# Layer 2 of a four-layer kernel: rows 0 and 32 of the spectrum packed into one, two columns per transform over h

## The chip, the core and the metric

The kernel runs on one core of a Trainium2 chip. The core has a matrix engine, TensorE (PE in the profile; PEld is its loading of stationary operands), a vector engine, VectorE (DVE), a scalar engine, ScalarE (ACT), GpSimd (POOL) and SyncE (SP), which issues most transfers. Each engine works through its own instructions in order and waits for the others by semaphores. Working data lie in SBUF, in 128 partitions; PE writes to PSUM, [...]and another engine copies the result from there. The metric is the device time of one execution in microseconds (us).

## The reference, cut to what matters

Four layers follow one another, each of the form x = x + L(group norm of x), on x of shape (2, 128, 64, 64) in float32: layer 0 has two attentions, layer 1 convolutions, layer 2 a quaternion convolution in the spectrum, layer 3 an attention. The change is in layer 2 alone:

```python
xs = jnp.stack([x[:, :q], x[:, q:2 * q], x[:, 2 * q:3 * q], x[:, 3 * q:]])
Xs = jnp.fft.rfft2(xs, s=(64, 64), axes=(-2, -1))
Ws = jnp.stack([kr_w + 1j * ki_w, kr_x + 1j * ki_x, kr_y + 1j * ki_y, kr_z + 1j * ki_z])
C = jnp.einsum('piohw,qbihw->pqbohw', Ws, Xs)
Pw = C[0, 0] - C[1, 1] - C[2, 2] - C[3, 3]
...
P = jnp.stack([Pw, Px, Py, Pz])
o = jnp.fft.irfft2(P, s=(64, 64), axes=(-2, -1))
```

Here q is 32. The spectrum has 64 rows (frequencies over h) and 33 columns (over w). Each of its points has its own 32x32 matrices, in eight arrays, so the layer reads 67.6 MB of weights.

## The kernel before

Layer 2 is `_layer2`. Each engine keeps the order in which the program issues (`_in_order`). There are three stages.

**Stage A, the transforms over h.** For each of the two images, `columns(i)` takes four columns of x: ACT normalizes them into `g` (L825), PE transposes two at a time (L831), DVE copies the result into `gt` (L837). `transformed(i, gt)` multiplies by `k["fwd_h"]` (L843), which makes, for each column, cosine and sine sums for rows 0 to 32 of the spectrum: 66 numbers. DVE copies them into `y` (L850), a tile that holds both images as (row, cosine or sine, column). `_skewed` issues the first function for group i+1 ahead of the second for group i.

**Stage B, the blocks.** As x is real, the transform over h of row 64 - m is the conjugate of that of row m, so 33 rows serve for all 64. Eight blocks (`kb`) take four rows each, and each block has two halves: the products with the weights of rows m (direct) and with those of rows 64 - m (image). `spectra(kb)` names the block's rows; the last block has five, as row 32 has only a direct half and row 0 only an image half. For a row, `transposed` has PE turn `y` (L872) and ACT copy it to `yt` (L878), and the second `transformed` multiplies by `k["fwd_w_both"]` (L885), which gives the transform over w for both halves. `placed` copies these to the tile `e` of a half with the signs of the quaternion product: twelve small copies per row, on ACT for one of two rows (L914) and on DVE for the other (L916). `products` multiplies by the weights (L975): 17 steps of four products on 32 columns of PE each. DVE transposes the results (L984) and adds them into `pz` (L992). `turned` transposes `pz` (L1004) and copies it to `pzt` on ACT (L1011), and `back` transforms back over w (L1027 and L1030, L1039 for row 0), with DVE's copies to `y` (L1032, L1040), where the results replace the inputs.

`alongside` runs one half's `products` and, between its steps, a queue of side work: generators that issue a piece each time they are called. In the first half of a block the queue is `turned` for the image half of the block before, `back` for that block, and `begun`: the first two rows of the next block, copied to its image tile only. In the second half it is `ended`: the same two rows copied to the direct tile, `turned` for the direct half, and the other rows into both tiles. The weights of a half are two transfers of 2112 KB on SP's queue (L789) into one of two buffers, so they are issued when the half two before has ended. The tiles of PSUM with the tag `bank` have two buffers, shared by `transposed`, `turned`, `back` and the last product step.

**Stage C, the transforms back over h.** `turned_back(i)` has PE transpose `y` for four columns (L1117), each to 66 partitions, and ACT copies to `zt` (L1124). `added(i, zt)` multiplies by `k["inv_h"]` (L1130), 66 rows by 64 columns, and DVE adds to x (L1134). In the second image, the statistics of the first image for layer 3 are made alongside: `steps` issues one piece per group (L1351 and the lines after).

Of the kernel before, what the change touches and what calls it, by code (L numbers as in the profile page):

```python
# [18 lines left out]
CH = 512  # L19
# [10 lines left out]
def _blocks():  # L30
# [11 lines left out]
    ang = 2 * np.pi * np.outer(np.arange(H), np.arange(FH)) / H  # L42
    k["fwd_h"] = np.kron(np.eye(2), np.concatenate([np.cos(ang), -np.sin(ang)], 1))
# [3 lines left out]
    k["fwd_w_both"] = np.zeros((2, W, 2, FW + 1, 2))  # L47
    for image, sign in enumerate((1, -1)):
        k["fwd_w_both"][0, :, image, :FW, 0] = c
        k["fwd_w_both"][0, :, image, :FW, 1] = -s  # L50
        k["fwd_w_both"][1, :, image, :FW, 0] = sign * s
        k["fwd_w_both"][1, :, image, :FW, 1] = sign * c
    k["fwd_w_both"] = k["fwd_w_both"].reshape(2 * W, 4 * (FW + 1))
# [4 lines left out]
    inv = np.stack([np.concatenate([c, s], 1), np.concatenate([-s, c], 1)], 1).reshape(2 * FW, 2 * W)  # L58
    k["inv_w"] = inv
    k["inv_w_mirror"] = inv * np.repeat([1.0, -1.0], W)  # L60

    ang = 2 * np.pi * np.outer(np.arange(FH), np.arange(H)) / H
    k["inv_h"] = np.stack([np.cos(ang), -np.sin(ang)], 1).reshape(2 * FH, H) / (H * W)
# [705 lines left out]
def _layer2(ctx, tc, X, weights, cst, src, here=None, there=None):  # L769
# [24 lines left out]
    y = one.tile([128, B, FH, 2, W], F32, name="y")  # L794
    with tc.tile_pool(name="l2_a", bufs=3) as ap, tc.tile_pool(
# [18 lines left out]
        for b in range(B):  # L814
# [8 lines left out]
            def columns(i):  # L823
                g = ap.tile([128, 4, H], F32, name="g")
                nc.scalar.activation(  # L825
                    g, xw[:, 4 * i : 4 * i + 4, :], AF.Identity, bias=shift, scale=scale
                )
                next(steps, None)
                pt = aps.tile([128, CH], F32, tag="pt", name="ps_pt")
                for n in range(2):  # L830
                    nc.tensor.transpose(  # L831
                        pt[:, n * 128 : (n + 1) * 128],
                        g[:, 2 * n : 2 * n + 2, :].rearrange("p w h -> p (w h)"),
                        ident,
                    )
                gt = ap.tile([128, 256], F32, name="gt")
                nc.vector.tensor_copy(gt, pt[:, :256])  # L837
                return gt

            def transformed(i, gt):  # L840
                py = aps.tile([128, CH], F32, tag="py", name="ps_py")
                for n in range(2):
                    nc.tensor.matmul(  # L843
                        py[:, n * 4 * FH : (n + 1) * 4 * FH],
                        gt[:, n * 128 : (n + 1) * 128],
                        k["fwd_h"],
                        start=True,
                        stop=True,
                    )
                nc.vector.tensor_copy(  # L850
                    y[:, b, :, :, 4 * i : 4 * i + 4].rearrange("p f c w -> p w c f"),
                    py[:, : 8 * FH].rearrange("p (w c f) -> p w c f", w=4, c=2),
                )

            _skewed(columns, transformed, W // 4)

    two = ctx.enter_context(tc.tile_pool(name="l2_two", bufs=2))
    with tc.tile_pool(name="l2_e", bufs=3) as ep, tc.tile_pool(
# [6 lines left out]
        def spectra(kb):  # L865

            return [4 * kb + 1 + j for j in range(4)] + [0] * (kb == BLOCKS2 - 1)

        def transposed(m):
            pt = bank()  # L870
            for b in range(B):
                nc.tensor.transpose(  # L872
                    pt[:, b * 128 : (b + 1) * 128],
                    y[:, b, m, :, :].rearrange("p c w -> p (c w)"),
# [6 lines left out]
        def transformed(yt):  # L881

            pe = bank("pe")
            for b in range(B):
# [3 lines left out]
                    k["fwd_w_both"],  # L888
# [5 lines left out]
        def placed(kb, m, got, image, e, scalar):  # L894
# [3 lines left out]
            if image:  # L898
                if m == FH - 1:
                    return  # L900
                s, row = (1, 4 * kb + 4 - m) if m else (0, 0)
            else:
                if not m:
                    return
                s, row = 0, m - 4 * kb - 1
# [31 lines left out]
        def rows_in(kb, rows, places, es, yts=None):  # L937

            if yts is None:
                yts = [transposed(m) for m in rows]  # L940
                yield
            gots = [transformed(yt) for yt in yts]
# [75 lines left out]
        def back(kb, direct, image):  # L1018

            for b in range(B):  # L1020
                pq = bank()
                for j in range(4):
                    m = 4 * kb + 1 + j
                    both = m != FH - 1
                    to = pq[:, j * 128 : (j + 1) * 128]
                    lhs = direct[b][:, j].rearrange("p r o -> p (r o)")
                    nc.tensor.matmul(to, lhs, k["inv_w"], start=True, stop=not both)  # L1027
                    if both:
                        lhs = image[b][:, 3 - j].rearrange("p r o -> p (r o)")
                        nc.tensor.matmul(to, lhs, k["inv_w_mirror"], start=False, stop=True)  # L1030
                m = 4 * kb + 1
                nc.vector.tensor_copy(  # L1032
                    y[:, b, m : m + 4, :, :].rearrange("p m c w -> p (m c w)"), pq
                )
                yield
                if kb == BLOCKS2 - 1:
                    pq = bank()
                    lhs = image[b][:, 0].rearrange("p r o -> p (r o)")
                    nc.tensor.matmul(pq[:, :128], lhs, k["inv_w"], start=True, stop=True)  # L1039
                    nc.vector.tensor_copy(  # L1040
                        y[:, b, 0, :, :].rearrange("p c w -> p (c w)"), pq[:, :128]
                    )
                    yield
# [1215 lines left out]
```

## Time and profile before

The times of three runs and of the profiled execution:

| what | us |
|---|---|
| median of three runs | 4382.42 |
| the three runs | 4372.78 to 4385.77 |
| the profiled execution | 4377.08 |
| its span, first to last instruction | 4375.3 |
| layer 2, stage A (1962.38 to 1999.92) | 37.5 |
| layer 2, stage B (2000 to 2278.85) | 278.9 |
| layer 2, stage C (2278.85 to 2359.60) | 80.8 |

The rest of the span belongs to the other three layers. The profile gives, for each engine, the time it was busy, the time it was idle before an instruction, and which instruction of which engine released it. PE's clock is not constant: the profile has the share of full clock that was granted, and shows it per window. A float32 product appears as two records of PE (two passes), a transpose as one.

```profile
PE 4128.4 (94%) x35988; PEld 1595.2 (36%) x35988; DVE 2203.8 (50%) x2410; ACT 3353.7 (77%) x4080; POOL 68.0 (2%) x145
PEclk9999999999999999999985999999999999999999
```

The second of these lines has one digit per fortieth of the span, in tenths of full clock; the digits 8 and 5 at the twenty-first and twenty-second place are layer 2's stage C and its neighbours.

### The profile page before, as it was taken

What the parts mean: (1) busy time and instruction counts of PE and PEld (TensorE: products, weight loads), DVE (VectorE), ACT (ScalarE), POOL (GpSimd) and SP (SyncE); (2) the same over time, 40 slices, a digit from 0 to 9 for tenths busy, and PEclk for the clock granted to TensorE, in tenths of its full rate; (3) what the DMA queues carried; (4) which work ended last, traced back from release to release, by engine and by line L of the source; (5) the groups of instructions that cost most, each with busy time, mean ns of one, the idle gap of its engine ahead of it and who ended that gap; (6) DMA issues with size and microseconds to landing.
All of it is one profiled execution on the core that took longest, in us unless ns stands there. A gap on an engine that the chain in (4) does not pass through costs nothing.

```text
span 4375.3 us, 82819 instructions
## 1 busy us (share of the span) xinstructions
PE 4128.4 (94%) x35988; PEld 1595.2 (36%) x35988; DVE 2203.8 (50%) x2410; ACT 3353.7 (77%) x4080; POOL 68.0 (2%) x145
## 2 busy tenths in 40 slices
PE   6899999979999997988887999999999999999998
PEld 3422222245222224445566333333333333333332
DVE  3579999736899998987753111222122212211111
ACT  3378888734888884226442999999999999999998
POOL 1001000000000001000000000000000000000000
PEclk9999999999999999999985999999999999999999
DMA  9996000000000000004640000000000000000000
GB/s 213 191 192 88 1 1 1 1 1 2 1 1 1 1 1 7 1 24 185 272 160 8 4 6 6 4 6 6 6 4 6 6 6 6 4 6 6 6 6 4
DMA packets 158826, 158.67 MB, mean 36 GB/s; under 512 B 24810, under 2 KB 148714, under 8 KB 154355
## 3 DMA queue, kind: packets, MB, share of 16 engines
q1 hardware_dynamic: 158450, 153.27, 14.8%
q8 instruction: 284, 4.65, 0.4%
q14 instruction: 92, 0.75, 0.1%
HBM read 144.85 MB, written 73.40 MB: 50 GB/s over the span
## 4 chain that ended last, share of the span: by engine, by line
PE 82%; DVE 13%; ACT 3%; issue 1%; POOL 0%; DMA 0%; SPq 0%; DVEq 0%; ACTq 0%; POOLq 0%
PE ps_acc L2057 23%; PE ps_s L2038 19%; PE ps_s L1313 13%; PE ps_acc L1726 12%; DVE X L649 4%; PE ps_sp L1517 4%; PE ps_z L975 2%; DVE sums L1761 1%; DVE e L916 1%; PE ps_po L1130 1%; PE ps_sp L1495 1%; PE ps_acc L1992 1%; ACT weights L1322 1%; PE ps_pt L1117 1%; PE ps_acc L1966 1%
## 5 line engine op out<-in xcount | busy, mean ns | idle before, releaser
L2048 ACT ACTIVATE weights<-ps_s 128x1024 f32<-128x1024 f32 x2048 | 1888.0, 1086 | 64.3 <-PE ps_s L2038 61.5
L1322 ACT ACTIVATE weights<-ps_s 128x1024 f32<-128x1024 f32 x1024 | 992.5, 1022 | 174.1 <-PE ps_s L1313 149.1
L2057 PE MATMUL ps_acc<-weights,vt 128*32 128x512 f32 x8192 | 1094.3, 606 | 0.0
L2038 PE MATMUL ps_s<-q,k 32*128 32x512 f32 x8192 | 932.6, 446 | 8.9 <-ACT weights L2048 8.9
L1761 DVE TENSOR_TENSOR sums<-sums,weights 128x2048 f32<-128x2048 f32 x384 | 879.1, 2289 | 42.1 <-ACT weights L1322 6.2
L2038 PEld LDWEIGHTS ps_s<-q,k 32*128 32x128 f32 x8192 | 472.5, 183 | 848.9 <-ACT weights L2048 788.6
L1313 PE MATMUL ps_s<-q,k 32*128 32x512 f32 x4096 | 645.8, 641 | 3.6 <-ACT weights L1322 2.2
L2079 DVE COPY u<-ps_acc 128x512 f32<-128x512 f32 x32 | 22.1, 691 | 1066.3 <-PE ps_acc L2057 1066.3
L1726 PE MATMUL ps_acc<-weights,vt 128*32 128x512 f32 x4096 | 548.9, 605 | 3.4 <-ACT used L1751 3.2
L1313 PEld LDWEIGHTS ps_s<-q,k 32*128 32x128 f32 x4096 | 209.7, 183 | 429.8 <-issue 212.5
L2057 PEld LDWEIGHTS ps_acc<-weights,vt 128*32 128x32 f32 x8192 | 163.0, 108 | 380.0 <-issue 368.0
L1726 PEld LDWEIGHTS ps_acc<-weights,vt 128*32 128x32 f32 x4096 | 81.0, 108 | 395.7 <-issue 377.6
L649 DVE SCALAR_TENSOR_TENSOR X<-g,w,X 128x2048 f32<-128x2048 f32 x84 | 197.3, 2350 | 2.4
L1517 PE MATMUL ps_sp<-pad,diag 32*32 32x512 f32 x4608 | 172.2, 609 | 11.2 <-issue 5.6
L1761 DVE TENSOR_TENSOR sums<-weights 128x2048 f32<-128x2048 f32 x64 | 146.5, 2289 | 61.4 <-ACT weights L1322 61.4
L1999 DVE TENSOR_TENSOR vt<-ps_acc,bv 128x384 f32<-128x384 f32 x32 | 17.8, 557 | 293.3 <-PE ps_acc L1992 293.3
L975 PE MATMUL ps_z<-w_ri,e 128*32 128x128 f32 x2048 | 138.1, 407 | 10.3 <-DVE e L916 5.3
L1517 PEld LDWEIGHTS ps_sp<-pad,diag 32*32 32x32 f32 x4608 | 93.5, 104 | 77.6 <-issue 32.5
L1495 PE MATMUL ps_sp<-xn,w_qkv 128*128 128x512 f32 x160 | 89.2, 695 | 32.6 <-DVE k L1528 15.2
L2082 DVE RECIPROCAL r<-r 128x512 f32<-128x512 f32 x32 | 107.3, 3353 | 1.1
L914 ACT ACTIVATE e<-ps_pe 32x136 f32<-32x136 f32 (+1 forms) x363 | 102.0, 281 | 4.2
L916 DVE TENSOR_SCALAR e<-ps_pe 32x136 f32<-32x136 f32 (+1 forms) x341 | 101.1, 297 | 4.7
(290 smaller groups left out, 2689.3 us busy)
## 6 DMA issues: line engine op xcount, KB each, us to landing
w_ri<-w_r SPq DMA_DIRECT2D x16, 2112.0 KB, 8.1
w_ri<-w_i SPq DMA_DIRECT2D x16, 2112.0 KB, 13.4
w_r<-in_L_conv_kr_w SPq DMA_DIRECT2D x15, 528.0 KB, 12.4
w_r<-in_L_conv_kr_x SPq DMA_DIRECT2D x15, 528.0 KB, 12.1
w_r<-in_L_conv_kr_y SPq DMA_DIRECT2D x15, 528.0 KB, 12.0
w_r<-in_L_conv_kr_z SPq DMA_DIRECT2D x15, 528.0 KB, 12.1
w_i<-in_L_conv_ki_w SPq DMA_DIRECT2D x15, 528.0 KB, 12.4
w_i<-in_L_conv_ki_x SPq DMA_DIRECT2D x15, 528.0 KB, 11.9
```

The source lines that it names most:

```text
L649: nc.vector.scalar_tensor_tensor(xi, g[:, i : i + H // 2, j : j + W], w8[:, s : s + 1], xi, ALU.mult, ALU.add)
L916: nc.vector.tensor_scalar_mul(out, got[of, :, s], sign)
L975: nc.tensor.matmul(out.rearrange("p (n f o) -> p n f o", n=2, f=2), e[:, s, 2 * j : 2 * j + 2, :].rearrange("p f x -> p (f x)"), w.rearran ...
L1313: nc.tensor.matmul(ps[j // 2][:, j % 2, :], k[rows, kt * 128 : (kt + 1) * 128], q[rows, qb * CH : (qb + 1) * CH], start=True, stop=True,)
L1322: nc.scalar.activation(w[:, 2 * p : 2 * p + 2, :], ps[p], AF.Exp)
L1495: nc.tensor.matmul(ps[:, i // ROWS, : rows * W], w_qkv[:, grp * C : (grp + 1) * C], xn[:, (first + r0 + i) * W : (first + r0 + i + rows) * W],
L1517: nc.tensor.matmul(ps[r // 2][to, r % 2, :].rearrange("p (h w) -> p h w", w=W), diag[rows, grp, t, :], pad[rows, y0 : y0 + ROWS, t % 3 : t ...
L1726: nc.tensor.matmul(ac[n][rows, :], lhs(rows), w[:, j, :], start=first, stop=last)
L1761: nc.vector.tensor_add(parts[0].rearrange("p j c -> p (j c)"), t.rearrange("p j c -> p (j c)"), w.rearrange("p j c -> p (j c)"),)
L2038: nc.tensor.matmul(ps[j // 2][:, j % 2, :], k[rows, kt * 128 : (kt + 1) * 128], q[n][rows, qb * CH : (qb + 1) * CH], start=(n == 0), stop= ...
L2048: nc.scalar.activation(w[p], ps[p], AF.Exp)
L2057: nc.tensor.matmul(ac[0][32 * j : 32 * j + 32, :], vt[:, kt, j // 2, i : i + 2, :].rearrange("p a d -> p (a d)"), w[j // 2][:, i, :], star ...
```

## The change

Rows 0 and 32 are real after the transform over h: their sines vanish. So they share one place. `fwd_h` now makes 64 numbers per column: row 0's cosine sum, row 32's in the place of row 0's sine, and cosine and sine for rows 1 to 31. Two columns fill 128 partitions, both on the way there and on the way back. `y` becomes (column, cosine or sine, row), with 32 rows.

The groups of stages A and C take eight columns in place of four, `steps` is called twice per group, and the copy to `y` in stage A goes to ACT. In stage B every block has four rows. The packed one is number 0; it has its own matrix forward (`fwd_w_ends`) and two on the way back (`inv_w_32`, `inv_w_0`). Each half now prepares two rows of the next block, for both tiles, ahead of `turned` and `back`; `e` has four buffers for three. The copies to `y` in `back` go to ACT, one per image and block, two in the last block.

```diff
-    k["fwd_h"] = np.kron(np.eye(2), np.concatenate([np.cos(ang), -np.sin(ang)], 1))
+    over_h = np.stack([np.cos(ang), -np.sin(ang)], 1)
+    over_h[:, 1, 0] = np.cos(np.pi * np.arange(H))
+    k["fwd_h"] = np.kron(np.eye(2), over_h.reshape(H, H))
...
+    k["inv_h"] = np.kron(np.eye(2), over_h.reshape(H, H).T / (H * W))
...
-    y = one.tile([128, B, FH, 2, W], F32, name="y")
+    y = one.tile([128, B, W, 2, FH - 1], F32, name="y")
...
-                g = ap.tile([128, 4, H], F32, name="g")
+                g = ap.tile([128, 8, H], F32, name="g")
                 nc.scalar.activation(
-                    g, xw[:, 4 * i : 4 * i + 4, :], AF.Identity, bias=shift, scale=scale
-                )
-                next(steps, None)
+                    g, xw[:, 8 * i : 8 * i + 8, :], AF.Identity, bias=shift, scale=scale
+                )
+                for _ in range(2):
+                    next(steps, None)
...
-                for n in range(2):
+                for n in range(4):
                     nc.tensor.transpose(
...
-                gt = ap.tile([128, 256], F32, name="gt")
-                nc.vector.tensor_copy(gt, pt[:, :256])
+                gt = ap.tile([128, CH], F32, name="gt")
+                nc.vector.tensor_copy(gt, pt)
...
-                nc.vector.tensor_copy(
-                    y[:, b, :, :, 4 * i : 4 * i + 4].rearrange("p f c w -> p w c f"),
-                    py[:, : 8 * FH].rearrange("p (w c f) -> p w c f", w=4, c=2),
-                )
-
-            _skewed(columns, transformed, W // 4)
+                for n in range(4):
+                    cols = slice(n * 128, (n + 1) * 128)
+                    nc.tensor.matmul(py[:, cols], gt[:, cols], k["fwd_h"], start=True, stop=True)
+                nc.scalar.copy(
+                    y[:, b, 8 * i : 8 * i + 8, :, :].rearrange("p w c f -> p (w c f)"), py
+                )
+
+            _skewed(columns, transformed, W // 8)
...
-    with tc.tile_pool(name="l2_e", bufs=3) as ep, tc.tile_pool(
+    with tc.tile_pool(name="l2_e", bufs=4) as ep, tc.tile_pool(
...
-            return [4 * kb + 1 + j for j in range(4)] + [0] * (kb == BLOCKS2 - 1)
+            return [(4 * kb + 1 + j) % (FH - 1) for j in range(4)]
...
-                    y[:, b, m, :, :].rearrange("p c w -> p (c w)"),
+                    y[:, b, :, :, m].rearrange("p w c -> p (w c)"),
...
-                    k["fwd_w_both"],
+                    k["fwd_w_both" if m else "fwd_w_ends"],
...
-                nc.vector.tensor_copy(
-                    y[:, b, m : m + 4, :, :].rearrange("p m c w -> p (m c w)"), pq
-                )
+                for lo, hi in ((0, 4),) if kb < BLOCKS2 - 1 else ((0, 3), (3, 4)):
+                    m = (m0 + lo) % (FH - 1)
+                    nc.scalar.copy(
+                        y[:, b, :, :, m : m + hi - lo].rearrange("p w c m -> p (w c) m"),
+                        pq[:, lo * 128 : hi * 128].rearrange("p (m x) -> p x m", m=hi - lo),
+                    )
...
+            side, n = [], 0
+            if nxt:
+                side.append(rows_in(kb + 1, nxt[:2], (1, 0), es))
+                n += 8
             if before:
-                side, n = [turned(pzs[1], before[1]), back(kb - 1, *before)], 7
+                side += [turned(pzs[1], before[1]), back(kb - 1, *before)]
+                n += 6
             else:
-                side, n = [rows_in(0, first[i : i + 2], (1,), e) for i in (0, 2)], 10
+                side = [rows_in(0, first[i : i + 2], (1,), e) for i in (0, 2)] + side
+                n += 10
+            alongside(products(rows_of_weights(kb, False), e[0], pzs[0]), chain(*side), n)
+            side, n = [turned(pzs[0], direct)], 4
             if nxt:
-                side.append(begun())
-                n += 5
-            alongside(products(rows_of_weights(kb, False), e[0], pzs[0]), chain(*side), n)
-            side, n = turned(pzs[0], direct), 4
-            if nxt:
-                side, n = ended(), 14
-            alongside(products(rows_of_weights(kb, True), e[1], pzs[1]), side, n)
+                side = [rows_in(kb + 1, nxt[2:], (1, 0), es)] + side
+                n += 8
+            alongside(products(rows_of_weights(kb, True), e[1], pzs[1]), chain(*side), n)
...
+                    w = 8 * i + 2 * n
                     nc.tensor.transpose(
-                        pt[: 2 * FH, n * 128 : (n + 1) * 128],
-                        y[:, b, :, :, 4 * i + n].rearrange("p f c -> p (f c)"),
+                        pt[:, n * 128 : (n + 1) * 128],
+                        y[:, b, w : w + 2, :, :].rearrange("p w c f -> p (w c f)"),
                         ident,
                     )
-                next(steps, None)
-                zt = cp.tile([2 * FH, 4, 128], F32, name="zt")
-                nc.scalar.copy(zt.rearrange("p i c -> p (i c)"), pt[: 2 * FH, :])
+                for _ in range(2):
+                    next(steps, None)
+                zt = cp.tile([128, CH], F32, name="zt")
+                nc.scalar.copy(zt, pt)
...
-                    nc.tensor.matmul(
-                        po[:, n * H : (n + 1) * H], zt[:, n, :], k["inv_h"], start=True, stop=True
-                    )
-                dst = xi[:, :, 4 * i : 4 * i + 4]
-                nc.vector.tensor_add(
-                    dst, po[:, : 4 * H].rearrange("p (w h) -> p h w", w=4), dst
-                )
+                    cols = slice(n * 128, (n + 1) * 128)
+                    nc.tensor.matmul(po[:, cols], zt[:, cols], k["inv_h"], start=True, stop=True)
+                dst = xi[:, :, 8 * i : 8 * i + 8]
+                nc.vector.tensor_add(dst, po.rearrange("p (w h) -> p h w", w=8), dst)
...
-            _skewed(turned_back, added, W // 4)
+            _skewed(turned_back, added, W // 8)
```

## The prediction, made before the changed kernel was run

> **What bounds the kernel now.** I read the page's first two parts first: TensorE (PE) is busy 94% of the 4375.3 us span. The windows of 10 us then place layer 2 between 1962 and 2360 us. It has three stages: the transforms over h (A, 1962.38 to 1999.92), the blocks (B, 2000 to 2278.85) and the transforms back over h (C, 2278.85 to 2359.6). Nothing outside them is edited. Two of those windows, one from A and one from C (after the range: its length, the busy us of PE, PEld, DVE, ACT and POOL, the granted clock, DMA):
>
> ```profile
> 1990.00:2000.00 10.00, 9.27 (x66) 7.47 (x65) 9.44 (x23) 5.98 (x8) 0.00 (x0) 1.00 0.02 3
> 2290.00:2300.00 10.00, 10.00 (x50) 9.61 (x49) 1.85 (x5) 2.32 (x4) 0.00 (x0) 0.50 0.01 2
> ```
>
> C is bound by PE, at half clock although PE never rests. The chain of waits gives its period, one group of four columns (start, length, what):
>
> ```profile
> 2284.67 0.82 PEld L1117 LDWEIGHTS ps_pt<-consts,y 128*66 128x66 f32 x4
> ...
> 2285.09 0.85 PE ps_pt L1117 x4
> 2285.95 1.60 PE ps_po L1130 x8
> ```
>
> Four transposes at 0.213 us and eight passes at 0.200 (each f32 product is two passes), 2.45 us. The eight stream only 64 columns each, but load 128 weight columns; the load sets their pace.
>
> A is bound by ACT and VectorE (DVE) alike. The groups by line:
>
> ```profile
> L825 ACT ACTIVATE g<-X,shift,st 128x256 f32<-128x256 f32 x32 | 25.0, 823 | 49.5 <-DVE shift L817 44.5 <-PE ps_pt L831 4.7
> L850 DVE COPY y<-ps_py 128x264 f32<-128x264 f32 x32 | 19.3, 604 | 2.8 <-PE ps_py L843 2.2
> L837 DVE COPY gt<-ps_pt 128x256 f32<-128x256 f32 x32 | 13.0, 405 | 2.6 <-PE ps_pt L831 2.6
> ```
>
> ACT does only `g`, and runs ahead. In B I read the windows between two `pz` of one block, then the timeline. First half of block, second half:
>
> ```profile
> 2078.34:2098.27 19.93, 18.12 (x219) 11.89 (x223) 11.47 (x29) 6.89 (x21) 0.00 (x0) 0.91 0.54 210
> 2098.27:2111.20 12.93, 9.47 (x132) 5.41 (x124) 12.40 (x35) 10.64 (x36) 0.00 (x0) 1.00 0.89 346
> ```
>
> In the second half DVE is busy 96% and PE waits for it; in the first DVE rests 8.5 us and PE carries the back transforms. The second half prepares three of a block's four sets of row copies (two rows into one of `e`'s two tiles), the first half one. What PE then waits for:
>
> ```profile
> 2079.64 0.60 PE L1004 MATMUL ps_bank<-consts,pz 128*66 128x128 f32 x4 [2.82 <-DVE pz L992]
> ```
>
> **Part 1, stage C.** A group becomes eight columns, 16 groups in place of 32, with the same 4 transposes and 8 passes, now all 128x128. At half clock: 12 x 0.213 = 2.56 us, in all 41 against 78.4. At full clock 12 x 0.107 = 1.28, with small gaps 1.32, in all 21. So the clock decides. The Trainium skill ("TensorE: Matmul & The Clock Gate", Part 1) says that the clock opens after some 3.4 us of activity and closes after an idle window; by it C would already run open, and the row says 0.50. So what counts is not PE's busy share. Streamed columns times filled rows fit: per group in C the transposes stream 4 x 0.213 us and the products 8 x 0.107 us on 66 of 128 rows, 1.29 of 2.45 us at half clock, 26% of what the open array does. In windows cut at the clock's own changes (every 3.41 us) that measure reached about 28 to 32% where the clock closed or stayed shut, and 39% or more where it opened or stayed open. The new C fills all rows: 50% even at half clock, so it opens within two windows. A rule speaks against this: the same page (Part 4) says that transposes do not engage the full clock, which would leave 41 us. Stage A has the same share, one transpose to two passes, and ran at 1.00 in the row above; I follow the row. New C: 21 + 2 (cold start) + 2 (first and last group) + 3 (in the second image eight `gn_st` of 0.676 share DVE with adds of about 0.69, so DVE needs 2.0 us per group for some groups against PE's 1.32, and PE's statistics products queue behind) + 1.5 for what I miss = 30. **Gain 51**, 35 if the clock stays shut. DVE and ACT (`zt` 0.58) are below 1.32 otherwise.
>
> **Part 2, stage A.** Eight groups per image for 16. PE's passes fall from 6 per four columns to 12 per eight: none gained there. DVE loses `y` (32 x 0.604) and gets `gt` of 512 columns, about 0.69 (the 128x512 copy of `y` from PSUM, L1032), so it is no bound. But `y` goes to ACT, in program order: g0 g1 y0 g2 y1 ... PE's order is T(i+1), M(i). So y(i) waits for M(i), which stands behind T(i+1), which needs g(i+1), and g(i+2) is queued behind y(i). ACT and PE now alternate; neither overlaps the other. One round:
>
> - `g` of 512. The skill ("ScalarE: Activation LUTs", What ACT_TABLE_LOAD costs: 186 ns + 0.833 per element, 93 per pointer operand) would make it 0.80 us, and today's 0.585. The row has 0.823, since the read strides over rows. The nearest 512-column row, L597 `gw` with a strided read, has 1.151, without pointers; I take 1.35 (1.25 to 1.5).
> - to PE and T, M: 12 passes, 1.28 us open or 2.56 shut; to ACT about 0.3 (L1117 to `zt`: 1.17 us for four passes of 0.213).
> - `y` 0.59.
>
> That is 3.6 us open, 4.9 shut. The measure above gives 26% shut and 36% open, so it sits under or near the threshold; I take 4.4. An image: 1.35 + 7 x 4.4 + 2 = 34.2, two 68.4, against 37.5 now. **Loss 31** (19 to 39). The larger constants' load precedes the first products by two `g` and is hidden.
>
> **Part 3, stage B.** Each half now prepares two sets of copies, before `turned` and `back` in its queue; the copies of `y` in `back` go from DVE to ACT. Per half, DVE: 2 x 3.75 of `e` (0.36 + 11 x 0.31), 3.15 of `z`, 1.15 of `pz` = 11.8. PE: 136 product passes x 0.0525 = 7.1, transposes and transforms 1.8, `turned` 1.2 = 10.1, and 4.1 more of `back` in the first half. ACT: 7.2 + 0.75 + 1.2, and two `y` copies in the first half. These now write runs of four: between 0.58 (the permuting `pzt` copy) and 1.15 (`gw`), I take 0.9; the second of a block's two is seen by the next half's transposes (two `bank` buffers), 0.7 us. Laid out in order: the first half ends with `back` at about 15.3; in the second the first `e` starts 3.2 us in (transposes, `yt`, transform), and the next half's first products wait for its last `e`: 13.0. A block takes 28.3 for 32.9 now, six such blocks give 27. The fifth row of the last preparation (PE idle from 2241.0 to 2244.4) goes, 3 more. **Gain 30.** Weights, 13.3 us from issue to landing, are issued when a half's products end and needed one half later, so DMA is next in line but not late. The `pz` stall goes, since `turned` now follows the copies; what is late next is the last `e` copy on DVE. Reading `y` with a stride when loading weights costs nothing that L1117, with a stride now, would show.
>
> **Sum.** -51 + 31 - 30 = -50. The profiled execution took 4377.1 us (span and 1.8 around it) and becomes 4327; the median of the runs is 5.3 above it, so I say **4332**.
>
> **Rivals.**
> - *As summed, 4332* (own range 4315 to 4350): 0.60.
> - *C stays shut* (the rule on transposes holds): -35 + 31 - 30 = -34, 4348. For it: C's whole 80 us at 0.50. Against: A. 0.12.
> - *A stays open* with `g` at its low end: 3.5 us per round, loss 18, 4319. For it: A's first image held 1.00 with PE resting a third of the time. 0.14.
> - *B gains nothing*, since in-order waits on two PSUM buffers (`pzt` behind eight `e` copies on ACT) replace the DVE wait: 4362. 0.10.
> - *Slower*: ACT's scattered copies in `back`. They hold the two banks and stand on the path from one half to the next. At 0.9 us each they cost what I counted; 16 of them decide at 0.9 + 50/16, 4 us each; at 5 us it is 4397. No ACT copy in the trace is over 1.2 us for 512 columns. 0.04.
>
> That the change does not do what it says is hardly a case: the new kernel's instruction streams have ACT's order as given above and two sets of copies per half.
>
> The range 4304 to 4364 takes in the own ranges of the first four. About 0.3% (13 us) is what can be told from no change: faster 0.91, same 0.05, slower 0.04.
>
> **What would show it.** C at clock 1.00 from its second window, 1.3 us per group (2.6: the second case). In A, ACT idle before `y`, released by PE, and PE idle before T, released by ACT `g`, rounds of 3.6 to 4.9 us. In B, `pz` spaced about 15 and 13 us, no idle before `turned` from `pz`. It is wrong if `g` is well over 1.5 us, or if B's period stays at 33.

## The result and the profile after

The changed kernel takes **4336.16 us** (median of 4 runs, 4332.12 to 4342.54), beside 4383.3 us for the kernel before: ratio 0.9898, 95% interval 0.9878 to 0.9918, 1% faster. The profiled execution took 4336.11 us (span 4334.3), 41.0 less than the one before. The medians are 47.1 apart, since the profiled execution before was 6 us under its median and this one is at it.

The windows below cut layer 2 of the changed kernel at its stages: A, then B in three parts (block 0 with the preparation ahead of it, the six blocks between the last `pz` of block 0 and that of block 6, the rest), then C. After the range come its length, the busy us (and count) of PE, PEld, DVE, ACT and POOL, the granted clock, the DMA share and GB/s.

```profile
1965.88:2020.95 55.07, 28.86 (x196) 25.31 (x197) 16.66 (x30) 27.85 (x32) 0.55 (x1) 0.91 0.40 167
2020.95:2075.39 54.44, 35.67 (x362) 23.73 (x362) 35.93 (x109) 32.74 (x110) 0.00 (x0) 0.78 0.24 89
2075.39:2258.44 183.05, 172.12 (x2064) 116.44 (x2062) 135.43 (x373) 115.02 (x348) 0.00 (x0) 0.93 0.72 285
2258.44:2291.60 33.16, 27.59 (x353) 19.39 (x353) 9.55 (x16) 6.39 (x12) 0.00 (x0) 0.95 0.28 117
2291.60:2318.20 26.60, 22.87 (x196) 21.94 (x196) 16.51 (x30) 9.28 (x16) 0.99 (x4) 1.00 0.00 1
```

The same cuts of the kernel before:

```profile
1962.38:1999.92 37.54, 31.46 (x196) 25.96 (x196) 31.98 (x78) 25.01 (x32) 0.55 (x1) 0.91 0.58 240
1999.92:2045.14 45.22, 34.16 (x360) 20.78 (x360) 33.64 (x100) 32.75 (x110) 0.00 (x0) 0.89 0.31 117
2045.14:2243.19 198.05, 167.82 (x2058) 105.20 (x2058) 141.95 (x380) 104.28 (x333) 0.00 (x0) 0.93 0.66 261
2243.19:2278.85 35.66, 29.58 (x364) 20.39 (x365) 12.72 (x22) 8.00 (x23) 0.00 (x0) 0.95 0.27 114
2278.85:2359.60 80.75, 80.30 (x388) 76.35 (x388) 19.43 (x46) 18.61 (x32) 0.75 (x2) 0.50 0.00 1
```

Set against each other, in us:

| stage | before | after | difference | predicted |
|---|---|---|---|---|
| A | 37.54 | 55.07 | +17.5 | +31 |
| B, block 0 | 45.22 | 54.44 | +9.2 | not priced |
| B, six blocks | 198.05 | 183.05 | -15.0 | -27 |
| B, the rest | 35.66 | 33.16 | -2.5 | -3 |
| C | 80.75 | 26.60 | -54.2 | -51 |

The differences add to -44.9. Layer 2 also starts 3.5 us later (1965.88 for 1962.38), behind code that nothing edits, which leaves -41.4; -41.0 was measured. So the total was close while two terms were off, and the errors cancelled.

**C** begins with the clock open and holds it. The timeline has one group in 1.34 us, from add to add:

```profile
2294.56 0.59 ACT L1099 COPY zt<-ps_pt 128x512 f32<-128x512 f32 x1 [1.20 <-PE ps_pt L1091]
...
2295.45 0.69 DVE L1108 TENSOR_TENSOR X<-ps_po,X 128x512 f32<-128x512 f32 x1 [0.57 <-PE ps_po L1106]
...
2296.79 0.69 DVE L1108 TENSOR_TENSOR X<-ps_po,X 128x512 f32<-128x512 f32 x1 [0.64 <-PE ps_po L1106]
```

**A** has the loop through ACT. In the groups by line, PE idles 26.3 us ahead of the transposes, released by `g`, and ACT 27.2 us ahead of `y`, released by PE's products. Each rests while the other works. Behind the first bar of a row stand the busy time and the mean length of one in ns, behind the second the idle time ahead of the group and what ended it:

```profile
L832 ACT ACTIVATE g<-X,shift,st 128x512 f32<-128x512 f32 x16 | 19.8, 1251 | 40.9 <-DVE shift L824 40.9
L839 PE MATMUL ps_pt<-consts,g 128*128 128x128 f32 x64 | 11.4, 305 | 26.3 <-ACT g L832 26.3
L853 ACT COPY y<-ps_py 128x512 f32<-128x512 f32 x16 | 9.4, 586 | 27.2 <-PE ps_py L852 27.2
```

The clock was mostly open (0.91). A round took 3.37 us at full clock (`y` at 1985.46 and 1988.83) and 4.65 at half (1970.69 and 1975.34).

**B**: the wait of `turned` for `pz` has nearly gone, from 22.7 us to 4.8 over the stage, and what is left falls behind the six blocks. A new one stands at 4.8: PE waits in `back` for ACT to copy `y` out of the `bank` buffer that it needs next. The first row is of the kernel before, the others of the changed one:

```profile
L1004 PE MATMUL ps_bank<-consts,pz 128*66 128x128 f32 x128 | 24.3, 325 | 22.7 <-DVE pz L992 22.7
L999 PE MATMUL ps_bank<-consts,pz 128*66 128x128 f32 x128 | 20.3, 283 | 4.8 <-DVE pz L987 4.8
L1024 PE MATMUL ps_bank<-consts,pzt 66*128 66x128 f32 x256 | 35.2, 295 | 5.1 <-ACT y L1027 4.8 <-ACT pzt L1006 0.2
```

The six blocks took 29.1 to 31.7 us each, 30.5 on average. The granted clock of 0.93 says that there are still windows at half clock; the long blocks are those that contain one.

### The profile page after: what moved, and what is told of

Same layout as the page of the kernel before. It is cut to its first block, busy times and chain, and to the rows that moved or that the text cites. A ratio compares the mean times of both kernels' runs of the same rounds, so it can differ in the third digit from the quotient of the medians.

```text
span 4334.3 us, 82274 instructions
## 1 busy us (share of the span) xinstructions
PE 4080.3 (94%) x35790; PEld 1559.5 (36%) x35790; DVE 2178.7 (50%) x2340; ACT 3353.9 (77%) x4069; POOL 67.5 (2%) x145
```

## The experiments

Ten kernels tell the terms apart, and two more join what was gained. Stage lengths are from one profile each; times are medians, but for `c_rows16` and `c_rows128`, which ran once each.

### C: is it the filled rows, or the state in which the stage begins?

The kernel before, with six dense products put ahead of stage C (`before_awake`):

```diff
+        for _ in range(6):
+            pt = cps.tile([128, CH], F32, tag="pt", name="ps_wake")
+            nc.tensor.matmul(pt, ident, X[:, 0, :CH], start=True, stop=True)
         for b in range(B):
             xi = X[:, b, :].rearrange("p (h w) -> p h w", w=W)
```

> The kernel before with six products of 128 rows by 512 columns put ahead of stage C, whose results nobody reads; all else as before. Theory (two stable states: C is 26% of the open array at half clock but about 50% at full, so it stays where it starts; what the change gave C is mostly that): C runs at clock 1.00 to its end, at 1.2 to 1.4 us per group of four columns in place of 2.45; with some 10 us for the added products it takes 50 to 57 us and not 80.75, the kernel is 24 to 31 us faster than before. Rival (the fill itself decides, a group of 66 rows and 64 streamed columns cannot hold the full clock): the clock falls back to 0.50 within two windows (7 us), C takes 78 to 86 us, the time is within 6 us of before's or longer.

Measured: 4354.06 us, 29.6 less than the kernel before (ratio 0.9935, 0.9918 to 0.9951). The windows of this kernel: the added products, then C.

```profile
2283.39:2290.25 6.86, 6.86 (x14) 3.12 (x15) 0.00 (x0) 0.00 (x0) 0.00 (x0) 0.79 0.00 0
2290.25:2333.48 43.23, 42.21 (x389) 41.58 (x386) 19.45 (x46) 18.49 (x32) 0.75 (x2) 1.00 0.01 1
```

The same C, 66 rows and 64 streamed columns, holds 1.00 to its end once it starts there: 43.2 us for 80.75. Two states are stable, and the kernel before sat in the slow one. So of the 54.2 us that the change gave C, 37.5 (80.75 to 43.2) are the clock, which six products whose results nobody reads also buy, at a price of 6.9 us, and 16.6 (43.2 to 26.6) the packing.

Do filled rows count at all? The changed kernel with C's products run four times, on 16 rows and on all (`c_rows16`, `c_rows128`):

```diff
-                for n in range(4):
-                    cols = slice(n * 128, (n + 1) * 128)
-                    nc.tensor.matmul(po[:, cols], zt[:, cols], k["inv_h"], start=True, stop=True)
+                for n in range(16):
+                    cols = slice(n % 4 * 128, (n % 4 + 1) * 128)
+                    nc.tensor.matmul(po[:, cols], zt[:16, cols], k["inv_h"][:16], start=True, stop=True)
```

> The changed kernel with the products of stage C run four times over, each on the first 16 of the 128 rows only (so the transform back over h sums 16 of its 128 rows): 16 products of 128 columns per group, 4 transposes as they were. PE never rests in C. Theory (the clock follows streamed columns times filled rows: (4 + 32 x 16/128)/36 = 22% of the open array): the clock, open at C's start, falls to 0.50 within two windows of 3.4 us and stays there; 7.7 us per group, C takes 105 to 123 us. Rival (PE's busy share or streamed columns alone count, and before's C was slow because only 64 columns were streamed per load): clock 1.00, 3.9 us per group, C takes 60 to 66 us.

> The control of c_rows16: the same products four times over, on all 128 rows (the repeats overwrite, so the sums are whole). Both theories: clock 1.00, 3.9 us per group, C takes 60 to 66 us. If this is at half clock too, PE at full load is throttled for another reason and c_rows16 says nothing.

The first window is C on 16 rows; the two behind it are C on 128, its first 3.5 us and the rest:

```profile
2292.57:2423.94 131.37, 130.53 (x580) 122.94 (x580) 16.90 (x30) 9.38 (x16) 0.97 (x4) 0.50 0.00 1
```

```profile
2294.30:2297.80 3.50, 3.50 (x16) 3.23 (x17) 0.00 (x0) 1.17 (x2) 0.00 (x0) 0.51 0.00 0
2297.80:2363.14 65.34, 63.60 (x566) 62.97 (x565) 16.81 (x30) 8.21 (x14) 0.98 (x4) 1.00 0.00 1
```

The same instructions on the same columns: on 16 rows PE is busy 99% for 131 us and gets half clock throughout (8.2 us per group, somewhat over the 7.7 expected); on 128 rows it opens the clock within 3.5 us and keeps it (in all 68.8 us, above the 60 to 66 expected). Rows count. One limit: the clock was down at the start of C in both runs (on 128 rows it fell just as C began), so they show that work on 16 rows doesn't open it where work on 128 does, and not that 16 rows would have closed an open one.

### A: the loop, ACT's load, or the clock?

Three kernels change stage A alone. In `a_y_dve` the copy of `y` goes to DVE:

```diff
-                nc.scalar.copy(
+                nc.vector.tensor_copy(
                     y[:, b, 8 * i : 8 * i + 8, :, :].rearrange("p w c f -> p (w c f)"), py
                 )
```

> The changed kernel with one edit: in stage A the copy of y from PSUM goes to VectorE (DVE) and no longer to ScalarE (ACT). Theory (the loss in A is the loop g, T, M, y, g through ACT's order): ACT then does only g and runs ahead, no idle of ACT before y and little of PE before the transposes; a round falls from 3.4 us (open clock) to what DVE takes for two copies of 512 columns, about 1.4 us, plus the statistics of the other image, 2 us at most. A takes 33 us (30 to 37) where it took 55.1, and the kernel is 18 to 25 us faster than the changed kernel, about 4314. Rival (the groups of eight columns are slow for another reason: g at 1.25 us, PE's passes at half clock, statistics on DVE): A stays above 47 us, the kernel gains under 8 us.

Measured: 4310.87 us (ratio to before 0.9834, 0.9817 to 0.985), 25.3 less than the changed kernel. A, to the end of its last `y` copy, takes 34.2 us, 3.3 less than before the change. ACT's wait for PE has shrunk to 3.6 us and PE's wait for `g` to 5.1; window of A and groups:

```profile
1967.49:2001.73 34.24, 26.80 (x196) 24.91 (x196) 26.29 (x46) 19.34 (x16) 0.55 (x1) 0.90 0.65 269
```

```profile
L832 ACT ACTIVATE g<-X,shift,st 128x512 f32<-128x512 f32 x16 | 19.3, 1265 | 52.0 <-DVE shift L824 48.4 <-PE ps_pt L839 3.6
L839 PE MATMUL ps_pt<-consts,g 128*128 128x128 f32 x64 | 11.2, 303 | 5.2 <-ACT g L832 5.1
```

This removes the loop and ACT's second job at once. Two more leave `y` on ACT and change the order alone; for that `columns` and `transformed` are each split in two (`turned` has the transposes, `stored` the copy of `y`). `a_order` puts the products ahead of the transposes:

```diff
...
-            _skewed(columns, transformed, W // 8)
+            gt = None
+            for i in range(W // 8 + 1):
+                g = columns(i) if i < W // 8 else None
+                py = transformed(i - 1, gt) if i else None
+                gt = turned(g) if g is not None else None
+                if i:
+                    stored(i - 1, py)
```

> The changed kernel with stage A's instructions in another order and nothing else: in each round g(i+1) on ScalarE (ACT), then the products M(i) on PE, then the transposes T(i+1), then the copy y(i), still on ACT. So M(i) no longer stands behind T(i+1), and y(i) is ready when g(i+1) ends. Theory (the loss in A is the loop in the order, g to T to M to y to the next g): a round falls to ACT's own work, 1.25 + 0.59 = 1.84 us, A takes 32 to 37 us where it took 55, and the time is near that of a_y_dve, 17 to 24 us faster than the changed kernel. Rival (ACT with both g and y is the bound, or the clock): A takes 45 us or more, the gain is under 10 us.

**A miss**: 4341.03 us (4334.08 to 4348.67), no gain. A to its last `y` copy is 56.9 us. The groups of stage A say why:

```profile
L855 PE MATMUL ps_py<-consts,gt 128*128 128x128 f32 x128 | 28.3, 390 | 12.8 <-DVE gt L848 12.8
L859 ACT COPY y<-ps_py 128x512 f32<-128x512 f32 x16 | 9.4, 586 | 28.9 <-PE ps_py L855 28.9
```

The products now wait for `gt`, the copy of the transposes directly in front of them: PE, DVE, PE is the new loop. The clock opened in the first image, at 1985.6 us, and rounds fell from 3.72 to 2.5 us; after the gap between the images (PE rests from 1996.9 to 1998.7) it closed again, at 1999.2, and the second image stayed at 0.50 to its end:

```profile
2000.00:2028.80 28.80, 22.58 (x92) 19.48 (x92) 4.90 (x8) 11.60 (x14) 0.00 (x0) 0.50 0.00 1
```

My order had taken one wait away and made another; so a third kernel, `a_ahead`, keeps PE's order of transposes before products and issues `g` one group earlier:

```diff
...
-            _skewed(columns, transformed, W // 8)
+            n = W // 8
+            gs = [columns(0), columns(1)]
+            gt = turned(gs[0])
+            for i in range(n):
+                if i + 2 < n:
+                    gs.append(columns(i + 2))
+                after = turned(gs[i + 1]) if i + 1 < n else None
+                stored(i, transformed(i, gt))
+                gt = after
```

> The changed kernel with stage A's g one group further ahead and nothing else: ACT's order is g(i+2), y(i), PE's is T(i+1), M(i) as in the changed kernel; y stays on ACT. In a_order M(i) stood right behind T(i) and waited for gt on DVE, which made another loop (T, gt, M, y), and it ran mostly at half clock. Here no engine waits for what the same round starts. Theory (the loss in A is the order, not ACT's load): a round falls to ACT's 1.25 + 0.59 = 1.84 us with the clock open, 2.6 to 2.8 us (PE's 12 passes) while it is shut; A takes 32 to 42 us, 14 to 23 us faster than the changed kernel, 4313 to 4322. Rival (two kinds of work on ACT, or the clock, hold A whatever the order): A takes 50 us or more, the gain is under 6 us.

Measured: 4317.26 us (ratio to before 0.9848, 0.9832 to 0.9865), 18.9 less than the changed kernel, with `y` still on ACT. The window of A, and ACT's rows in a stretch of its second image:

```profile
1966.62:1999.32 32.70, 25.14 (x196) 22.19 (x196) 16.36 (x30) 27.60 (x32) 0.55 (x1) 1.00 0.68 282
```

```profile
1993.02 1.28 ACT L832 ACTIVATE g<-X,shift,st 128x512 f32<-128x512 f32 x1
...
1994.29 0.59 ACT L859 COPY y<-ps_py 128x512 f32<-128x512 f32 x1
...
1994.77 1.28 ACT L832 ACTIVATE g<-X,shift,st 128x512 f32<-128x512 f32 x1
```

Neither row has an idle time in brackets: ACT works without a rest, 1.75 us per round. So the loss in A was the order of instructions. That ACT has two jobs costs nothing that shows in the stage: with `y` on DVE it took 34.2 us, 1.5 more than here, at a clock of 0.90 for 1.00. The times of the two kernels (4310.87 and 4317.26) have intervals that overlap.

### B: what keeps a block from 28.3 us?

`b_rows128` pads the spectra with zeros, so that `back` contracts over 128 rows for 66; `inv_w` and its three relatives get 62 rows of zeros as well:

```diff
-                        pt[: 2 * FW, r * 128 : (r + 1) * 128],
-                        pz[:, r * B + b, :FW, :].rearrange("p f c -> p (f c)"),
+                        pt[:, r * 128 : (r + 1) * 128],
+                        pz[:, r * B + b, :, :].rearrange("p f c -> p (f c)"),
...
-            two.tile([128, 4 * B, 2 * PAIRS, 2], F32, name=f"pz{n}", bufs=1) for n in range(2)
+            two.tile([128, 4 * B, 64, 2], F32, name=f"pz{n}", bufs=1) for n in range(2)
```

> The changed kernel with the spectra of the products padded by zeros from 66 to 128 rows, so that the transforms back over w (back) contract over 128 rows and not 66; the number of passes and the output are the same. Theory (the clock follows streamed columns times filled rows, and back with 66 rows falls under it): no block has a window at half clock any more, the granted clock of the six blocks goes from 0.93 to 0.98 or more, their mean period from 30.5 to 29.0 or 29.5 us; in all 7 to 14 us faster. Rival (only streamed columns or PE's busy share count, not rows): clock 0.93 as it was, the period within 0.3 us, the time unchanged or up to 3 us longer for the wider loads of the transposes.

Measured: 4330.18 us (4322.85 to 4337.61), 6.0 less than the changed kernel; the two intervals against before (0.9867 to 0.9904 here) overlap, so the stage decides. The six blocks of this kernel:

```profile
2071.05:2247.56 176.51, 165.92 (x2063) 111.97 (x2062) 135.41 (x373) 115.08 (x348) 0.00 (x0) 0.99 0.75 296
```

Five of the six took between 29.16 and 29.19 us, as the changed kernel's two blocks without a half-clock window did (29.1); the first, which has one, took 30.65. Multiplying by zeros keeps the clock open; the passes are the same in number, and the price shows nowhere.

`back_dve` takes the `y` copies in `back` off ACT:

```diff
-                    nc.scalar.copy(
+                    nc.vector.tensor_copy(
                         y[:, b, :, :, m : m + hi - lo].rearrange("p w c m -> p (w c) m"),
```

> The changed kernel with one edit: the copies of y in back go to VectorE (DVE) again, as before the change, and no longer to ScalarE (ACT). Theory (a first half has room on DVE, 11.8 of 16.4 us; B's gain is the even halves, and the PE waits for y come from two bank buffers and the clock): six blocks take 183 us within 3, the kernel's time within 4 us of the changed kernel's. Rival (DVE freed of the y copies is what buys the shorter block): two copies of 0.69 us more per block, the six blocks 6 to 10 us longer.

**A miss for both**: 4325.21 us (4316.63 to 4333.52), 11.0 less than the changed kernel, where I had expected no difference and the rival a loss. Here too the intervals overlap a little (0.9845 to 0.9886), so the stage decides. Its six blocks, and in them the groups of `back` and of the products:

```profile
2073.77:2245.49 171.72, 164.42 (x2064) 110.16 (x2062) 143.15 (x384) 106.39 (x336) 0.00 (x0) 1.00 0.77 304
```

```profile
L1024 PE MATMUL ps_bank<-consts,pzt 66*128 66x128 f32 x192 | 24.6, 281 | 1.2 <-DVE z L979 1.2
L970 PE MATMUL ps_z<-w_ri,e 128*32 128x128 f32 x1536 | 102.5, 408 | 5.3 <-DVE e L912 5.3
```

Without the wait for ACT, PE's rest in `back` is short enough that the clock never falls, at 66 rows as before, and five blocks take 28.5 us each (the first 29.1). The three kernels split the block: 28.5 by its engines; about 0.7 more with the wait for ACT's copy (29.17 in `b_rows128`); 1.3 more with the half-clock windows that this wait lets in (30.5). The copy is no slower on ACT: 0.720 us there, 0.716 on DVE. What costs is its place in ACT's queue.

In this kernel the clock was down when C began, unlike in the changed kernel. The rest of B, the last part of it alone, then C:

```profile
2245.49:2281.77 36.28, 30.53 (x352) 22.27 (x353) 12.58 (x22) 3.40 (x6) 0.00 (x0) 0.85 0.25 108
2271.32:2281.77 10.45, 7.91 (x40) 7.41 (x41) 2.81 (x6) 1.07 (x2) 0.00 (x0) 0.64 0.01 2
2281.77:2312.60 30.83, 27.33 (x196) 26.37 (x196) 16.60 (x30) 9.27 (x16) 1.01 (x5) 0.85 0.00 1
```

C opened it again by itself, some 6 us after its start: its adds at 2285.75 and 2288.16 are 2.4 us apart, those at 2288.16 and 2289.50 only 1.3. The packed C does not stay shut. The shut clock cost 3.1 us in the rest of B and 4.2 in C against the changed kernel, so the profiled execution (4329.84) shows less of the blocks' 11.3 than the median does. This need not be the edit: `c_rows16` and `c_rows128` have the changed kernel's code up to C, and in both the clock was down at the start of C.

### Block 0

In the changed kernel the first half of block 0 prepares four sets of copies and its second half two. In that second half PE waits 7.2 us, in the timeline at the last of these rows:

```profile
2056.68 3.16 ACT L910 ACTIVATE e<-ps_pe 64x136 f32<-64x136 f32 x11
...
2060.24 3.16 ACT L910 ACTIVATE e<-ps_pe 64x136 f32<-64x136 f32 x11
2063.45 1.27 PE L887 MATMUL ps_pe<-consts,yt 128*128 128x136 f32 x4 [7.20 <-ACT e L910]
```

`b0_split` moves one set from the first half to the second:

```diff
-                side = [rows_in(0, first[i : i + 2], (1,), e) for i in (0, 2)] + side
+                side = [rows_in(0, first[i : i + 2], (1,), e) for i in (0, 2)] + [begun()]
...
+                if not before:
+                    side.insert(0, copies(1, nxt[:2], gots, (0,), es))
```

> The changed kernel with one edit in block 0 alone: its first half prepares three sets of copies and its second three, where it has four and two. Theory (block 0 lost 9 us to four sets standing in the first half's queues, with PE waiting for yt behind the e copies on ACT): the first half of block 0 falls from 54.4 us to 45 to 47 and the second grows by 0 to 3; in all 6 to 9 us faster than the changed kernel. Rival (the loss is the clock, 0.78 there, or work that only moves into the second half): block 0 as a whole within 3 us of 77.4 us (first half 54.4 and the second up to 2075.4 to 2088.8), no difference in the time.

**The theory fell**: 4337.92 us (4327.8 to 4345.26), block 0 53.2 us, and the same wait is still there. (The expectation took 54.4 us, the whole of block 0, for its first half; the halves were 31.9 and 22.6 us, and are 29.9 and 23.2 here.)

```profile
2064.00 1.27 PE L887 MATMUL ps_pe<-consts,yt 128*128 128x136 f32 x4 [7.18 <-ACT e L910]
```

The number of sets isn't it. `b0_order` keeps the split, and in the second half puts `turned` between the two preparations (shown against the changed kernel):

```diff
-            if nxt:
+            if nxt and before:
                 side = [rows_in(kb + 1, nxt[2:], (1, 0), es)] + side
                 n += 8
+            elif nxt:
+                side = [copies(1, nxt[:2], gots, (0,), es)] + side
+                side.append(rows_in(1, nxt[2:], (1, 0), es))
+                n += 11
```

> As b0_split (block 0 prepares three sets in each half), but in the second half of block 0 the spectra of the first (turned) now stand between the last copies of one pair of rows and the next pair's transposes. In b0_split PE's transform of the next pair waits 7.2 us there, until ACT has made both sets of e from the same ps_pe bank. Theory (block 0's loss is this order: two preparations back to back, with only two ps_pe banks and PE's products queued behind the waiting transform): the wait falls to under 2 us, the second half of block 0 (from the first half's pz to its own) from 23.2 to 15 to 18 us, the kernel is 5 to 8 us faster than b0_split. Rival (the half is bound by its sum of copies on ACT and DVE, or by the clock at 0.77): 21 us or more, within 2 us of b0_split.

The wait goes, and block 0 takes 45.4 us, as before the change; but block 1 takes 36.1 where it took 30.9, since its products now wait for `e`:

```profile
2026.39:2071.79 45.40, 34.08 (x358) 21.36 (x358) 33.63 (x100) 32.63 (x111) 0.00 (x0) 0.89 0.32 123
2071.79:2107.87 36.08, 30.68 (x348) 20.61 (x348) 24.91 (x70) 19.08 (x58) 0.00 (x0) 0.86 0.56 223
```

```profile
2075.49 0.64 PE L970 MATMUL ps_z<-w_ri,e 128*32 128x128 f32 x2 [4.53 <-DVE e L912]
```

Blocks 0 and 1 together fall from 85.3 us to 81.5, and the kernel's time, 4335.61 us (4321.09 to 4341.22), isn't told from the changed kernel's: in this profile A took 63.0 us. The expectation held for the half and failed for the sum. The windows of block 0 account for its 9.2 us: PE's idle time grew by 7.7 (54.44 - 35.67 for 45.22 - 34.16), of which 7.2 are this wait, and its busy time by 1.5, at a clock of 0.78 for 0.89. The other order takes the wait out of block 0 and brings 5.2 us back in block 1; an order that has neither was not found.

### Together

`best_a` joins `a_y_dve`, `back_dve` and `b_rows128`; `best_b` has the order of `b0_order` too.

> The changed kernel with three edits together: y copied by VectorE (DVE) in stage A (a_y_dve), y copied by DVE in back (back_dve), and the spectra padded to 128 rows (b_rows128). If the gains are of different places they add: A 30 us instead of 55; six blocks 171 to 172 us instead of 183 at clock 0.99 or more; C's first groups at an open clock, 26 to 27 us. In all 32 to 40 us faster than the changed kernel, 4297 to 4305. If the padding gives nothing where back_dve has opened the clock already, the blocks are as in back_dve and only the tail gains; if A's and B's edits collide on DVE, the sum is short by 8 us or more.

> best_a with block 0's other order (b0_order) as well. Theory (in b0_order the wait left block 0 and came back in block 1's first half, 36.1 for 30.9 us; of the loss of block 0 only part can be had): within 5 us of best_a, either way. Rival (with the y copies on DVE, ACT has room and the wait doesn't come back): 5 to 9 us faster than best_a.

`best_a` takes 4301.31 us (4295.45 to 4307.68; ratio to before 0.981, 0.9797 to 0.9823), 34.9 less than the changed kernel. A took 34.7 us (34.2 in `a_y_dve`), and not the 30 expected. The six blocks, the rest of B, and C of `best_a`:

```profile
2058.57:2231.40 172.83, 166.09 (x2063) 111.68 (x2062) 143.09 (x384) 106.52 (x336) 0.00 (x0) 0.99 0.76 302
2231.40:2264.80 33.40, 27.70 (x353) 19.57 (x353) 12.52 (x22) 3.43 (x6) 0.00 (x0) 0.95 0.27 116
2264.80:2293.03 28.23, 24.53 (x196) 23.60 (x196) 16.60 (x30) 9.18 (x16) 0.98 (x4) 0.94 0.00 1
```

The gains of `a_y_dve` and `back_dve` nearly add (25.3 and 11.0, of the 34.9). That of the padding does not come on top: the six blocks take 172.8 us, and 171.7 in `back_dve`, which has opened the clock already. C starts with the clock open. `best_b` takes 4300.55 us (4296.53 to 4305.79), no different. Its block 0 and its six blocks:

```profile
2000.77:2044.85 44.08, 32.69 (x358) 20.21 (x358) 33.63 (x100) 32.70 (x110) 1.32 (x2) 0.92 0.34 127
2044.85:2224.88 180.03, 169.25 (x2066) 113.89 (x2066) 145.40 (x392) 106.41 (x336) 0.00 (x0) 0.96 0.73 286
```

Block 0 gains and the blocks behind it lose, as in `b0_order`. Either kernel is faster than both kernels of the change.

## Why the prediction came out as it did

**C, gain 51: right, measured 54.2.** "The clock decides" held. The split went unsaid: I weighed the new C against the threshold and never asked whether the old one could have run open. By the same measure, about 50% at full clock, it could; `before_awake` did. The 2 us for a cold start weren't needed, since the tail of B left the clock open; in `back_dve` it was shut, and C opened it in some 6 us, within the two windows predicted. The row of stage A was the right one to follow, and not the Trainium skill ("TensorE: Matmul & The Clock Gate", Part 4), by which transposes do not engage the full clock: C, with one transpose to two passes, ran at 1.00.

**A, loss 31: mechanism right, size wrong, 17.5.** The loop was as drawn, with the two idle times and releasers named, and `a_ahead` and `a_y_dve`, at 32.7 and 34.2 us, show it to be the whole loss. The mis-sized term is the round: "I take 4.4", measured 3.37 with the clock open, 4.65 with it shut, and mostly open. I had put A's 36% of the open array "under or near the threshold"; it was open for most of the stage, shut only about the start of each image. This is the rival "A stays open" (3.5 us, loss 18). `g` was 1.251 us for 1.35, worth 1.6 us of the rest.

**B, gain 30: the step that failed, measured 8.3** (15.0 + 2.5 - 9.2). Two terms. "A block takes 28.3" was measured as 30.5. The layout by engines was nearly right, 28.5 in `back_dve`, and the wait for the last `e` that it put next is there (5.3 us over the six blocks, in the changed kernel as in `back_dve`). But it took the clock as open, and it moved the `y` copies to ACT at the price of their length and 0.7 us. The 0.7 was right and the length was over-priced (0.72 us for 0.9); what was left out is that the wait lets the clock fall, 1.3 us per block. The other term is block 0. The prediction priced "six such blocks" and nothing for the one in which two preparations follow each other with no `turned` and `back` between them; it lost 9.2 us, 7.2 of them in one wait.

**The sum** came within about 4 us by luck: A lost 13.5 us less than predicted, C gained 3.2 more, and B gained 21.7 less.

**The rivals.** "C stays shut" did not come. "B gains nothing" was right that a wait on the two `bank` buffers would take the place of the one for DVE, but it came in `back`, before the copies of `y`, and took only part of the gain. The slower one, ACT's copies in `back`, had its place right and its price wrong: the copy costs its 0.72 us, far from the 4 us at which it would decide, but ACT is still the wrong engine for it, by 11.3 us over the six blocks.

## What to carry to other kernels

When PE is at half clock and never idle, ask first whether the stage could hold full clock if it began there, before rebuilding it: a few dense products put ahead of it answer that in one run. A copy that moves to an engine which also starts the next round closes a loop; price the loop with the engines' orders written out, and check that a reordering doesn't close another. A block time put together from busy times needs the clock checked against the waits it contains, and the first block of a pipeline priced by itself.

## What the runs showed of the hardware

Filled rows count for the clock, and PE's busy share alone doesn't open it: 99% busy on 16 rows stayed at 0.50 for 131 us, the same products on 128 rows were at 1.00 after 3.5 us, and zeros in rows 66 to 127 raised the clock of B from 0.93 to 0.99.

Near the threshold, single windows decide. In the changed kernel's A the clock fell at 1969 and at 1996.2 us, around the thin start of each image, and opened again after one or two windows of 3.4 us, although a shut round of 4.65 us holds only 28% of the open array's work (12 passes of 0.107 us): its passes come in one burst, and a window with the whole burst has 38%. Its rounds of 3.37 us at full clock hold 38%, and kept it. `a_order`, shut at 3.72 us per round (34%), opened in its first image 10 us after it had fallen, and in the second stayed shut for the 28.8 us of its window. That agrees with the prediction's threshold between 32 and 39%; the same 34% with two outcomes says that averages over a round are too coarse a measure for A.

Work that thins when it slows down has two stable times: the old C was 26% shut and is about 50% open, and either lasted to its end. This may also be why kernels with the loop in A have a wide range (4321 to 4341 us for `b0_order`; 4315 to 4321 for `a_ahead`, which is without it); that their runs differ by the clock in A is an inference from profiles with A at 55 and 63 us, and wasn't tried.
